# Masked aggregation of thirteen tiles instead of seven, in float32r

## The chip, the cores and the metric

The kernel runs on one core of one Trainium2 chip. The metric is the device time of one launch in microseconds. Before the change it is 1266.72 us, the median of three runs (1264.11 to 1269.66).

## The reference

A graph has 4096 nodes with 512 features each, and an integer adjacency matrix of 4096 x 4096 that has some 2 ones in a thousand and a full diagonal. Two layers are computed, each on the normalised input:

```python
h = jnp.maximum(_layernorm(x, axis=-1), 0.0)
x = x + _L0_gnn_ref(h, adj, WQ, WK, WV, we, be)
h = jnp.maximum(_layernorm(x, axis=-1), 0.0)
x = x + _L1_gnn_ref(h, adj, W_self, b_self, W_nb, b_nb, W_comb, b_comb)

# layer 0: 8 heads; attn = Q K^T / 8 + energy, masked by adj, softmax
hard = (attn == jnp.max(attn, axis=-1, keepdims=True)).astype(jnp.float32) / HEADS
out = jnp.einsum('hqk,hkd->hqd', hard, V)

# layer 1
mask = (adj > 0).astype(x.dtype)
deg = jnp.sum(mask, axis=1, keepdims=True)
agg = mask @ x / jnp.maximum(deg, 1.0)
self_f = x @ W_self + b_self
nb_f = agg @ W_nb + b_nb
out = relu(jnp.concatenate([self_f, nb_f], axis=-1) @ W_comb + b_comb)
```

The change touches only the product `mask @ x` of layer 1.

## The kernel before

The kernel works on 32 tiles of 128 nodes and keeps a second, general path for graphs that are too dense; it isn't taken here. The path that runs has three stages.

**First stage.** The adjacency matrix is read. For each node, the 4096 bits of its row are packed by matmuls into 256 words of 16 bits; word j holds the bits of the nodes j, 256 + j, 512 + j and so on. The words go to DRAM (`W_d`), and from them a list of each node's neighbours is decoded. Keys and values of layer 0 go to DRAM (`K_d`). Nodes are then ranked by their number of neighbours, and `perm` gives the new order: tile 0 holds the nodes with the longest lists. `CAPS` has the longest list of each of the 32 tiles, self included: 24, 15, 14, 13, 12, 12, 12, 11, 11, 11, 10, 10, 10, 10, 9, 9, and so on down to 5.

**Second stage.** For each tile in the new order GpSimd gathers the keys of the neighbours with indirect DMAs, VectorE scores them, and the winners' values are gathered. Layer 1's weights are folded, so that what has to be summed over neighbours is one vector of 512 per node (`gs`), which is scattered by `perm` to DRAM (`G_d`). The node's own part and its new x go to `X1_d`. Near the end of the stage the words of the first tiles are gathered (`dense_words`), turned by TensorE and copied back as integers by VectorE (`dense_turn`).

**Third stage.** The neighbours' vectors are summed, in two ways.

The first seven tiles (`DENSE = 7`) are summed by TensorE, as a product of masks and keys. There are 16 steps (`NPL`), one for each bit of the words. In step s, `dense_mask` (L1656, VectorE) shifts and masks the words of all seven tiles so that a set bit becomes the fp32 number 2.0, `dense_keys` (L1665, ScalarE's queue) loads the 256 vectors of `G_d` that belong to that bit, and `dense_sum` (L1675, TensorE) adds seven tiles x two halves of fp32 matmuls, 128x128 by 128x512, into seven PSUM banks `da0` to `da6`. Masks and keys have three buffers each.

The tiles 7 to 31 are summed from gathers: GpSimd gathers one vector per neighbour slot and node (L1110, `room<-G_d,sidx`), into a ring of three tiles' room, and VectorE sums them with one reduction (`total`, L1697; for the last tile by halves, L1706). In `finish` (L1687, L1688, VectorE) a sum is scaled by the degree and added to the node's own part, and `put` scatters the finished rows to the output (L1126, GpSimd).

The order of all this is written out by hand; each engine executes its instructions in the order of the code. A loop goes over the tiles from 7 to 31. It counts GpSimd's calls and puts the next step's mask and matmuls into the order whenever the count has passed 13 more. The first three steps stand ahead of the loop. The seven TensorE tiles are finished in iterations 27 to 29. `load_x1` (L1682, SyncE's queue) brings each tile's own part, some tiles ahead.

Of the kernel before, what the change touches and what calls it, by code (L numbers as in the profile page):

```python
# [9 lines left out]
F32 = mybir.dt.float32  # L10
BF16 = mybir.dt.bfloat16
I32 = mybir.dt.int32
AF = mybir.ActivationFunctionType
ALU = mybir.AluOpType
AX = mybir.AxisListType
# [3 lines left out]
P = 128  # L19
# [493 lines left out]
LISTV = CAPS[VTILE]  # L513
FIRST = 4
GMAX = 10
DENSE = 7
MAGIC = 0x5F3759DF


# [18 lines left out]
def sparse_path(  # L538
# [560 lines left out]
    with ExitStack() as pb:  # L1099
# [321 lines left out]
            3: [(1, NC), (0, NC)],  # L1421
        }

        def dense_words():

            wg = gp.tile([P, DENSE, SEG], F32, tag="kg", name="wg")
            for r in range(DENSE):
                gather(wg[:, r, :], W_d[:, :], perm[:, r : r + 1])
            return wg

        def dense_turn(wg):

            wT = wp.tile([P, 2, DENSE, P], I32, tag="w_a", name="wT")
            for a in range(0, DENSE, 2):
                pt = pst.tile([P, NC, P], F32, tag="tr", name="tr")
                m = min(2, DENSE - a)
                for h in range(2):
                    for b in range(m):
                        nc.tensor.transpose(pt[:, 2 * h + b, :], wg[:, a + b, ts(h, P)], ident)
                nc.vector.tensor_copy(  # L1440
                    wT[:, :, a : a + m, :],
                    pt.rearrange("p (h b) q -> p h b q", h=2)[:, :, 0:m, :],
                )
            return wT
# [87 lines left out]
        for i in range(-5, KT):  # L1532


            if i == -3:
                load_fold(0)
            if i == 0:
                load_bias()
            if i == 1:
                wS = wp.tile([P, NC, D], F32, tag="w_b", name="swS")  # L1540
                wN = bp.tile([P, NC, D], F32, tag="swN", name="swN", bufs=1)
            a, b = on(key_gathers, i), late(value_gathers, "value", i)
            while a or b:
                for q, n in ((a, max(1, round(len(a) / max(1, len(b))))), (b, 1)):
                    for g in q[:n]:
                        gather(*g)
                    del q[:n]
            on(rows, i + 5)
            late(layer1_move, "move", i)
            on(query_copy, i + 2)  # L1550
            late(layer1_copy, "layer1", i)
            early = [r for r in tail if plan["turn"][r] == i - 1]
            for r in early:
                tail_turn(r)
            if i >= 0 and turns[i] in fused:
                own_values(turns[i])
            late(layer1_stats, "stats", i)
            on(query_norm, i + 4)
            on(query, i + 1)
            for part in between.get(i, ()):  # L1560
                fold(*part)
            late(layer1, "layer1", i)
            for r in early[: -1 if i == KT - 1 else None]:
                tail_product(r)
            if i in (-2, -1, 0):
                n = 2
                for t in late_v[:n]:
# [12 lines left out]
            if i >= 0:  # L1580
                scores(turns[i], within)
            if i == KT - 2:
                wg = dense_words()
            late(scatter, "move", i)
            if i == KT - 2:
                gsl = [gp.tile([P, GRP, D], F32, tag="kg", name="gs") for _ in range(2)]
            on(winners, i)
            late(layer1_norm, "stats", i)
            on(query_turn, i + 3)
            if i < KT - 1:  # L1590
                late(layer1_turn, "turn", i)
                for r in early:
                    tail_move(r)
# [11 lines left out]
        late(layer1_norm, "stats", KT)  # L1605
        for r in early[-1:]:
            tail_move(r)
        for r in at_end:
            layer1_turn(r)
            tail_turn(r)  # L1610
# [23 lines left out]
        nc.tensor.matmul(fps, fm, ones[:, 0:1], start=True, stop=True)  # L1634
        fi = cp.tile([1, 1], I32, tag="fi", name="fi")
        nc.vector.tensor_copy(fi, fps)
        wT = dense_turn(wg)
        for r in tail:
            s = st[r]
            s["pr"] = own_product(s)  # L1640
            layer1_out(r)


    with ExitStack() as pd:
        dp = pd.enter_context(tc.tile_pool(name="sd", bufs=4))
        gp = pd.enter_context(tc.tile_pool(name="sdg", bufs=3))
        psd = pd.enter_context(tc.tile_pool(name="spsd", bufs=1, space=PSUM))
        order = pd.enter_context(ExitStack())
        order.enter_context(tc.manual_schedule())
        dacc = [psd.tile([P, D], F32, tag=f"da{r}", name="da") for r in range(DENSE)]  # L1650
        masks, keys = {}, {}

        def dense_mask(s):

            mk = gp.tile([P, 2, DENSE, P], F32, tag="mk", name="mk")
            nc.vector.tensor_scalar(  # L1656
                mk.rearrange("p h b q -> p (h b q)").bitcast(I32),
                wT.rearrange("p h b q -> p (h b q)"), 22 - s, 0x40000000,
                ALU.logical_shift_left, ALU.bitwise_and,
            )  # L1660
            masks[s] = mk

        def dense_keys(s):
            gk = gp.tile([P, 2, D], F32, tag="gk", name="gk")
            nc.scalar.dma_start(  # L1665
                gk, G_d[ds(s * SEG, SEG), :].rearrange("(h p) f -> p h f", p=P)
            )
            keys[s] = gk

        def dense_sum(s):  # L1670
            todo = [(h, r) for h in range(2) for r in range(DENSE)]
            if s == NPL - 1:
                todo.sort(key=lambda hr: hr[1])
            for h, r in todo:
                nc.tensor.matmul(  # L1675
                    dacc[r], masks[s][:, h, r, :], keys[s][:, h, :],
                    start=(s == 0 and h == 0), stop=(s == NPL - 1 and h == 1),
                )

        def load_x1(r):  # L1680
            x1 = dp.tile([P, 2, D], F32, tag="x1", name="x1", bufs=DENSE + 5)
            nc.sync.dma_start(x1, X1_d[ts(r, P), :, :])  # L1682
            return x1

        def finish(r, acc, by, x1):
            x1, y = x1[:, 0, :], x1[:, 1, :]
            nc.vector.scalar_tensor_tensor(y, acc, by, y, ALU.mult, ALU.add)  # L1687
            nc.vector.scalar_tensor_tensor(y, y, 0.0, x1, ALU.max, ALU.add)  # L1688
            done.append((r, y))

        def put():
            put_rows(out[:, :], *done.pop(0))
# [17 lines left out]
            return g[:, 0, :]  # L1710


        half = cp.tile([P, DENSE], F32, tag="half", name="half")
        nc.vector.tensor_scalar(half, smeta[:, 0:DENSE, M_RD - M_DEG], 0.5, None, ALU.mult)
        done = []
        puts.clear()
        for s in range(NPL):
            dense_keys(s)
        ahead = 3
        for s in range(ahead):  # L1720
            dense_mask(s)
            dense_sum(s)
        s = ahead
        calls = 0

        pace = 13
        x1s = {}
        for r in range(DENSE, KT):
            n = CAPS[r] - 1
            for q in [*range(r, min(r + 4, KT)), *(range(DENSE) if r == KT - 6 else ())]:  # L1730
                if q not in x1s:
                    x1s[q] = load_x1(q)
            gg = room[:, ds(r % 3 * GMAX * D, GMAX * D)].rearrange("p (n f) -> p n f", f=D)
            for i in range(n):
                gather(gg[:, i, :], G_d[:, :], sidx[:, r, i + 1 : i + 2])

            for k in range(len(done) if r == KT - 1 else 2 if r in (KT - 3, KT - 2) else 1):
                if len(done) > (r < KT - 1):
                    put()
            acc = (total if r < KT - 1 else halved)(gg, n)  # L1740
            finish(r, acc, smeta[:, r, M_RD - M_DEG : M_RD + 1 - M_DEG], x1s.pop(r))

            for k in {KT - 5: (0, 1), KT - 4: (2, 3), KT - 3: range(4, DENSE)}.get(r, ()):
                finish(k, dacc[k], half[:, k : k + 1], x1s.pop(k))
            calls += n + 1
            while s < NPL and calls >= pace * (s - 2):
                dense_mask(s)
                dense_sum(s)
                s += 1
        assert s == NPL  # L1750
        while done:
            put()
        order.close()
# [47 lines left out]
```

## Time and profile before

| what | value |
|---|---|
| median of the runs (lowest, highest) | 1266.72 us (1264.11, 1269.66) |
| span of the profiled execution | 1448.9 us |
| the profiled execution's own time | the page gives its span only |
| mean granted TensorE clock in it | 0.841 |
| busy: PE, VectorE (DVE), ScalarE (ACT), GpSimd (POOL) | 72%, 68%, 29%, 53% of the span |
| DMA | 352.57 MB, mean 243 GB/s |
| third stage | from 1128.0 us (first mask) to 1448.9 us |
| ScalarE in the third stage | no busy time |

A line of a group reads: line of the code, engine, operation, output<-inputs, shapes, count | busy us, mean ns of one | idle time of the engine just before these, and what ended most of it. PE is TensorE's matmuls and PEld its weight loads; an fp32 matmul shows as two records of each. "Remote" and "issue" are waits that the profile can't put down to an instruction. SP is SyncE. "Clock" is the share of full speed that TensorE was granted.

### The profile page before, as it was taken

The page shows a single profiled execution, that of the slowest core. Times are in us where ns is not written, and L with a number is a line of the kernel's source. Part 1 is how long each engine was busy: PE and PEld are TensorE (multiplying, and loading weights), DVE is VectorE, ACT ScalarE, POOL GpSimd, SP SyncE. Part 2 cuts the span into 40 slices and gives each one's busy share as a digit, 9 for nine tenths or more (in the row PEclk, how much of TensorE's full clock was granted, in tenths as well). Part 3 has the DMA queues.
Part 4 walks back from the last instruction along what each step waited for, and adds up shares of the span by engine and source line. Part 5 has one row for each costly group of instructions (what it writes and reads, how often), then busy time and mean ns, then how long its engine had stood idle before and what let it go on. Part 6 is the DMA issues. An engine that isn't in the chain of part 4 may idle for free.

```text
span 1448.9 us, 10626 instructions
## 1 busy us (share of the span) xinstructions
PE 1041.9 (72%) x2852; PEld 478.2 (33%) x2852; DVE 991.3 (68%) x1622; ACT 426.9 (29%) x880; POOL 772.9 (53%) x913
## 2 busy tenths in 40 slices
PE   5998989877553662754877778777895779596590
PEld 3554545433221221321332323233341334142240
DVE  5568687970990884865976878677760839487476
ACT  5787667512100420332332333333430000000000
POOL 2322322426675666544666766666527375747473
PEclk9999999989785876876978879798998789687595
DMA  9999998397754577556677777766737886757572
GB/s 365 420 419 420 419 346 301 128 365 240 210 147 120 166 222 237 177 184 188 212 221 239 243 229 225 217 211 199 263 111 237 338 263 207 246 194 257 199 246 104
DMA packets 109974, 352.57 MB, mean 243 GB/s; under 512 B 18192, under 2 KB 18192, under 8 KB 101712
## 3 DMA queue, kind: packets, MB, share of 16 engines
q0 software_dynamic: 64128, 210.72, 46.0%
q1 hardware_dynamic: 39552, 129.78, 23.2%
q10 hardware_dynamic: 6224, 11.31, 2.3%
q8 instruction: 24, 0.39, 0.1%
q14 instruction: 46, 0.38, 0.1%
HBM read 287.74 MB, written 68.19 MB: 246 GB/s over the span
## 4 chain that ended last, share of the span: by engine, by line
PE 46%; issue 19%; DVE 12%; POOL 7%; another core or an unknown queue 6%; DMA 6%; ACT 2%; SPq 0%; POOLq 0%; DVEq 0%; ACTq 0%
PE da L1675 15%; PE pg L628 7%; PE pr L1367 6%; PE q L628 5%; POOL kg L1110 4%; PE pk L628 4%; PE pv L628 3%; DVE pr L1231 3%; PE pw L768 2%; PE pr L1365 2%; POOL o L1110 2%; DMA room<-adj_dram 2%; DVE sc L1234 1%; DMA K_d<-x_dram 1%
## 5 line engine op out<-in xcount | busy, mean ns | idle before, releaser
L1675 PE MATMUL da<-gk,mk 128*128 128x512 f32 x448 | 221.7, 645 | 83.6 <-issue 56.1
L628 PE MATMUL pg<-swN,hT 128*128 128x512 f32 x216 | 133.3, 774 | 124.7 <-issue 63.7
L1110 POOL DMA_INDIRECT room<-G_d,sidx x184 | 181.1, 984 | 57.8 <-issue 54.5
L1110 POOL DMA_INDIRECT kg<-K_d,sidx x177 | 167.5, 946 | 77.9 <-issue 56.3
L628 PE MATMUL q<-wq,hqT 128*128 128x512 f32 x256 | 137.9, 670 | 70.7 <-issue 67.0
L1234 DVE TENSOR_REDUCE sc<-pr 128x32 f32<-128x2048 f32 (+3 forms) x114 | 183.3, 1608 | 5.7 <-remote 1.8
L1697 DVE TENSOR_REDUCE acc<-room 128x512 f32<-128x4096 f32 (+5 forms) x24 | 161.1, 6711 | 2.0 <-DMA room<-G_d,sidx 2.0
L1675 PEld LDWEIGHTS da<-gk,mk 128*128 128x128 f32 x448 | 91.5, 205 | 213.9 <-issue 213.9
L1110 POOL DMA_INDIRECT o<-K_d,vi x128 | 122.5, 957 | 39.3 <-issue 38.1
L628 PE MATMUL pk<-wk,room 128*128 128x512 f32 x256 | 121.7, 620 | 3.9 <-ACT room L810 3.9
L628 PEld LDWEIGHTS pg<-swN,hT 128*128 128x128 f32 x216 | 53.5, 256 | 205.1 <-issue 136.9
L628 PE MATMUL pv<-wv,room 128*128 128x512 f32 x256 | 115.7, 603 | 0.1
L1110 POOL DMA_INDIRECT room<-K_d,sidx x102 | 97.1, 952 | 32.5 <-issue 28.6
L1231 DVE TENSOR_TENSOR pr<-q,kg 128x2048 f32<-128x2048 f32 (+3 forms) x51 | 102.4, 2007 | 2.0 <-DVE sc L1234 0.7
L1367 PE MATMUL pr<-swS,hT 128*128 128x512 f32 x216 | 99.9, 605 | 0.0
L1231 DVE TENSOR_TENSOR pr<-q,room 128x2048 f32<-128x2048 f32 (+3 forms) x42 | 66.7, 1589 | 45.7 <-remote 42.7
L1126 POOL DMA_INDIRECT G_d<-gs,perm x32 | 32.5, 1017 | 122.5 <-ACT gs L1373 91.9
L628 PEld LDWEIGHTS q<-wq,hqT 128*128 128x128 f32 x256 | 51.1, 210 | 130.2 <-issue 126.9
L749 ACT ACTIVATE mkt<-adjt,sgb 128x2048 bf16<-128x2048 int32 x37 | 74.3, 2008 | 11.8 <-POOL adjt L670 11.6
L1126 POOL DMA_INDIRECT out_dram<-x,perm x32 | 33.6, 1050 | 82.5 <-DVE x L1688 51.4
L1267 DVE COPY_PREDICATED o<-best,room 128x512 f32<-128x512 int32 x102 | 74.7, 732 | 3.5
L824 POOL DMA_DIRECT2D K_d<-ks x32 | 18.8, 588 | 96.1 <-DVE ks L819 92.5
(222 smaller groups left out, 1503.4 us busy)
## 6 DMA issues: line engine op xcount, KB each, us to landing
adjt<-adj_dram SPq DMA_DIRECT2D x37, 1024.0 KB
room<-adj_dram SPq DMA_DIRECT2D x27, 1024.0 KB
x<-X_d SPq DMA_DIRECT2D x32, 512.0 KB
xt<-x_dram SPq DMA_DIRECT2D x32, 256.0 KB
K_d<-ks POOLq DMA_DIRECT2D x32, 256.0 KB
X_d<-xo SPq DMA_DIRECT2D x32, 256.0 KB
X_d<-own SPq DMA_DIRECT2D x32, 256.0 KB
gk<-G_d ACTq DMA_DIRECT2D x16, 512.0 KB
```

The costliest lines, as they stand in the source:

```text
L628: nc.tensor.matmul(dst, h[:, c, :], w[:, c, :], start=(c == 0), stop=(c == NC - 1))
L749: nc.scalar.activation(mk, st[t]["adj"][j], AF.Sigmoid, bias=sgb, scale=400.0, accum_out=degs[:, t, j : j + 1],)
L768: nc.tensor.matmul(pw, planes[:, s, :], st[t]["mk"][j][:, ts(i, SEG)], start=False, stop=(s == NPL - 1),)
L1110: last[0] = nc.gpsimd.indirect_dma_start(out=dst, out_offset=None, in_=src, in_offset=bass.IndirectOffsetOnAxis(ap=idx, axis=0), element_o ...
L1126: new = nc.gpsimd.indirect_dma_start(out=dst, out_offset=bass.IndirectOffsetOnAxis(ap=perm[:, r : r + 1], axis=0), in_=src, in_offset=None,)
L1231: nc.vector.tensor_tensor(pr[:, :g, :], s["q"].unsqueeze(1).to_broadcast([P, g, D]), kk, ALU.mult)
L1234: nc.vector.tensor_reduce(sc[:, g0 : g0 + g, :], pr[:, :g, :].rearrange("p g (h d) -> p g h d", h=H), AX.X, ALU.add,)
L1267: nc.vector.copy_predicated(s["o"].rearrange("p (h d) -> p h d", h=H), best[:, k, :].bitcast(I32).unsqueeze(2).to_broadcast([P, H, HD]), b ...
L1365: nc.tensor.matmul(pr, ones[0:1, :], bb[0:1, :], start=True, stop=False)
L1367: nc.tensor.matmul(pr, s["hT1"][:, c, :], wS[:, c, :], start=False, stop=(c == NC - 1))
L1675: nc.tensor.matmul(dacc[r], masks[s][:, h, r, :], keys[s][:, h, :], start=(s == 0 and h == 0), stop=(s == NPL - 1 and h == 1),)
L1697: nc.vector.tensor_reduce(acc, g[:, 0:n, :].rearrange("p n f -> p f n"), AX.X, ALU.add)
```

## The change

Thirteen tiles instead of seven are summed by TensorE, in two passes over the 16 bits: tiles 0 to 6, then 7 to 12. The loop over gathered tiles starts at 13. There are 32 steps; in each the 256 keys of a bit are loaded (so each is loaded twice in all).

The matmuls are in float32r, a rounded fp32. Keys are split in two float32r parts: `hi` is a copy by ScalarE, `lo` is keys minus `hi` by VectorE, and each fp32 matmul becomes two float32r matmuls into the same bank. The mask is made by VectorE as integers, as before, into a tile of its own (`mi`), and copied by ScalarE to float32r (`mk`).

Key loads move from ScalarE's queue to SyncE's, three steps ahead; loads of x1 have 11 buffers, not 12. The words of the second group are gathered ahead of the last scatters of the second stage and turned behind the last own products. PSUM banks are reused: the second pass's tiles have the banks 7 and 0 to 4, so that the first pass's tiles are finished in steps 16 and 17. Steps are put into the order for every 4.6 calls of GpSimd, puts counted as calls, two steps ahead of the loop.

```diff
-DENSE = 7
+DENSE = (7, 6)
+DTILES = sum(DENSE)
...
+        def dense_words(k):
+            n, at = DENSE[k], k * DENSE[0]
+            wg = gp.tile([P, n, SEG], F32, tag="kg", name="wg")
+            for r in range(n):
+                gather(wg[:, r, :], W_d[:, :], perm[:, at + r : at + r + 1])
             return wg
...
             if i == KT - 2:
-                wg = dense_words()
+                wgs = [dense_words(0)]
...
         late(layer1_norm, "stats", KT)
         for r in early[-1:]:
             tail_move(r)
+        wgs.append(dense_words(1))
...
-        wT = dense_turn(wg)
+        wTs = [dense_turn(0, wgs[0])]
         for r in tail:
             s = st[r]
             s["pr"] = own_product(s)
             layer1_out(r)
+        wTs.append(dense_turn(1, wgs[1]))
...
-        gp = pd.enter_context(tc.tile_pool(name="sdg", bufs=3))
+        gp = pd.enter_context(tc.tile_pool(name="sdg", bufs=2))
...
+        def dense_mask(u):
+            k, s = divmod(u, NPL)
+            shape = [P, 2, DENSE[k], P]
+            mi = gp.tile(shape, I32, tag="mi", name="mi")
             nc.vector.tensor_scalar(
-                mk.rearrange("p h b q -> p (h b q)").bitcast(I32),
-                wT.rearrange("p h b q -> p (h b q)"), 22 - s, 0x40000000,
+                mi.rearrange("p h b q -> p (h b q)"),
+                wTs[k].rearrange("p h b q -> p (h b q)"), 22 - s, 0x40000000,
                 ALU.logical_shift_left, ALU.bitwise_and,
             )
+            mk = gp.tile(shape, F32R, tag="mk", name="mk", bufs=3)
+            nc.scalar.copy(
+                mk.rearrange("p h b q -> p (h b q)"),
+                mi.rearrange("p h b q -> p (h b q)").bitcast(F32),
+            )
+            masks[u] = mk
+
+        def dense_keys(u):
+            s = u % NPL
+            gk = gp.tile([P, 2, D], F32, tag="gk", name="gk", bufs=3)
+            nc.sync.dma_start(
                 gk, G_d[ds(s * SEG, SEG), :].rearrange("(h p) f -> p h f", p=P)
             )
+            keys[u] = gk
+
+        def dense_split(u):
+            gk = keys.pop(u)
+            hi = gp.tile([P, 2, D], F32R, tag="hi", name="hi")
+            nc.scalar.copy(hi, gk)
+            lo = gp.tile([P, 2, D], F32R, tag="lo", name="lo")
+            nc.vector.tensor_tensor(lo, gk, hi.bitcast(F32), ALU.subtract)
+            keys[u] = (hi, lo)
+
+        def dense_sum(u):
+            k, s = divmod(u, NPL)
+            at = k * DENSE[0]
+            if s == 0:
+                for r in range(DENSE[k]):
+                    dacc[at + r] = psd.tile([P, D], F32, tag=f"da{(at + r) % 8}", name="da")
+            todo = [(h, r) for h in range(2) for r in range(DENSE[k])]
             if s == NPL - 1:
                 todo.sort(key=lambda hr: hr[1])
+            mk, parts = masks.pop(u), keys.pop(u)
             for h, r in todo:
-                nc.tensor.matmul(
-                    dacc[r], masks[s][:, h, r, :], keys[s][:, h, :],
-                    start=(s == 0 and h == 0), stop=(s == NPL - 1 and h == 1),
-                )
+                for c, part in enumerate(parts):
+                    nc.tensor.matmul(
+                        dacc[at + r], mk[:, h, r, :], part[:, h, :],
+                        start=(s == 0 and h == 0 and c == 0),
+                        stop=(s == NPL - 1 and h == 1 and c == 1),
+                    )
...
+        def step(u):
+            dense_mask(u)
+            if u + 3 < STEPS:
+                dense_keys(u + 3)
+            dense_split(u)
+            dense_sum(u)
+            if u == NPL - 1:
+                for r in range(DENSE[0]):
+                    load_x1(r)
+            if u == NPL:
+                for r in range(0, 4):
+                    finish_dense(r)
+            if u == NPL + 1:
+                for r in range(4, DENSE[0]):
+                    finish_dense(r)
+            if u == STEPS - 2:
+                for r in range(DENSE[0], DTILES):
+                    load_x1(r)
+
+        for u in range(3):
+            dense_keys(u)
+        for r in range(DTILES, DTILES + 3):
+            load_x1(r)
+        step(0)
+        step(1)
+        u = 2
         calls = 0
-        pace = 13
+        pace = 4.6
-        for r in range(DENSE, KT):
+        for r in range(DTILES, KT):
             n = CAPS[r] - 1
...
+            while len(done) > (1 if r < KT - 1 else 0):
+                put()
+                calls += 1
             acc = (total if r < KT - 1 else halved)(gg, n)
...
+            calls += n
+            while u < STEPS and calls >= pace * (u - 2):
+                step(u)
+                u += 1
+            if r == KT - 2:
+                while u < STEPS:
+                    step(u)
+                    u += 1
+                for k in range(DENSE[0], DTILES):
+                    finish_dense(k)
```

More of the change, by code (lines that the diff above doesn't have):

```diff
@@ L12 @@
 I32 = mybir.dt.int32
+F32R = mybir.dt.float32r
 AF = mybir.ActivationFunctionType
@@ L1422, in sparse_path, with dense_turn @@
         }
[L1424 to L1428, printed above, removed]
-            return wg
-        def dense_turn(wg):
-            wT = wp.tile([P, 2, DENSE, P], I32, tag="w_a", name="wT")
-            for a in range(0, DENSE, 2):
+        def dense_words(k):
[3 more added lines that the diff above has]
+                gather(wg[:, r, :], W_d[:, :], perm[:, at + r : at + r + 1])
+            return wg
+        def dense_turn(k, wg):
+            n = DENSE[k]
+            wT = wp.tile([P, 2, n, P], I32, tag=("w_a", "w_b")[k], name="wT")
+            for a in range(0, n, 2):
                 pt = pst.tile([P, NC, P], F32, tag="tr", name="tr")
-                m = min(2, DENSE - a)
+                m = min(2, n - a)
                 for h in range(2):
@@ L1649, in sparse_path @@
         order.enter_context(tc.manual_schedule())
-        dacc = [psd.tile([P, D], F32, tag=f"da{r}", name="da") for r in range(DENSE)]
+        dacc = {}
         masks, keys = {}, {}
-        def dense_mask(s):
-            mk = gp.tile([P, 2, DENSE, P], F32, tag="mk", name="mk")
+        STEPS = 2 * NPL
+        def dense_mask(u):
+            k, s = divmod(u, NPL)
+            shape = [P, 2, DENSE[k], P]
+            mi = gp.tile(shape, I32, tag="mi", name="mi")
             nc.vector.tensor_scalar(
-                mk.rearrange("p h b q -> p (h b q)").bitcast(I32),
-                wT.rearrange("p h b q -> p (h b q)"), 22 - s, 0x40000000,
+                mi.rearrange("p h b q -> p (h b q)"),
+                wTs[k].rearrange("p h b q -> p (h b q)"), 22 - s, 0x40000000,
@@ L1659, in dense_mask @@
                 ALU.logical_shift_left, ALU.bitwise_and,
             )
[L1661 to L1665, printed above, removed]
+            mk = gp.tile(shape, F32R, tag="mk", name="mk", bufs=3)
[8 more added lines that the diff above has]
+            nc.sync.dma_start(
@@ L1666, in dense_keys @@
                 gk, G_d[ds(s * SEG, SEG), :].rearrange("(h p) f -> p h f", p=P)
             )
-            keys[s] = gk
-        def dense_sum(s):
-            todo = [(h, r) for h in range(2) for r in range(DENSE)]
+            keys[u] = gk
[6 more added lines that the diff above has]
+            keys[u] = (hi, lo)
@@ L1680, in load_x1, with finish @@
         def load_x1(r):
-            x1 = dp.tile([P, 2, D], F32, tag="x1", name="x1", bufs=DENSE + 5)
+            x1 = dp.tile([P, 2, D], F32, tag="x1", name="x1", bufs=11)
             nc.sync.dma_start(x1, X1_d[ts(r, P), :, :])
-            return x1
-        def finish(r, acc, by, x1):
+            x1s[r] = x1
+        def finish(r, acc, by):
+            x1 = x1s.pop(r)
             x1, y = x1[:, 0, :], x1[:, 1, :]
@@ L1689, in finish, with finish_dense @@
             done.append((r, y))
+        def finish_dense(r):
+            finish(r, dacc[r], half[:, r : r + 1])
         def put():
@@ L1710, in halved @@
             return g[:, 0, :]
-        half = cp.tile([P, DENSE], F32, tag="half", name="half")
-        nc.vector.tensor_scalar(half, smeta[:, 0:DENSE, M_RD - M_DEG], 0.5, None, ALU.mult)
+        half = cp.tile([P, DTILES], F32, tag="half", name="half")
+        nc.vector.tensor_scalar(half, smeta[:, 0:DTILES, M_RD - M_DEG], 0.5, None, ALU.mult)
         done = []
         puts.clear()
[L1717 to L1723, printed above, removed]
+        x1s = {}
+        def step(u):
[23 more added lines that the diff above has]
+        u = 2
         calls = 0
-        pace = 13
-        x1s = {}
-        for r in range(DENSE, KT):
+        pace = 4.6
+        for r in range(DTILES, KT):
             n = CAPS[r] - 1
-            for q in [*range(r, min(r + 4, KT)), *(range(DENSE) if r == KT - 6 else ())]:
-                if q not in x1s:
-                    x1s[q] = load_x1(q)
+            if r + 3 < KT:
+                load_x1(r + 3)
             gg = room[:, ds(r % 3 * GMAX * D, GMAX * D)].rearrange("p (n f) -> p n f", f=D)
@@ L1735, in sparse_path @@
                 gather(gg[:, i, :], G_d[:, :], sidx[:, r, i + 1 : i + 2])
-            for k in range(len(done) if r == KT - 1 else 2 if r in (KT - 3, KT - 2) else 1):
-                if len(done) > (r < KT - 1):
-                    put()
+            while len(done) > (1 if r < KT - 1 else 0):
+                put()
+                calls += 1
             acc = (total if r < KT - 1 else halved)(gg, n)
[L1741 to L1750, printed above, removed]
+            finish(r, acc, smeta[:, r, M_RD - M_DEG : M_RD + 1 - M_DEG])
+            calls += n
[8 more added lines that the diff above has]
+                    finish_dense(k)
         while done:
```

## The prediction

> **What bounds the kernel now.** I read the page first, then its last stage (from 1128 us, where masks, keys and final sums run) as groups, stretches, waits and timeline. The page says that the profiled execution has a span of 1448.9 us and no other time; that is 182.2 us above the median of the runs, 1266.72. So I ask at once what in it a shorter execution cannot hold.
>
> The groups of the last stage (count | busy us, mean ns | idle before):
> ```profile
> L1675 PE MATMUL da<-gk,mk 128*128 128x512 f32 x448 | 221.7, 645 | 83.6 <-issue 56.1 <-DMA gk<-G_d 27.5
> L1697 DVE TENSOR_REDUCE acc<-room 128x512 f32<-128x4096 f32 (+5 forms) x24 | 161.1, 6711 | 2.0 <-DMA room<-G_d,sidx 2.0
> L1126 POOL DMA_INDIRECT out_dram<-x,perm x32 | 33.6, 1050 | 82.5 <-DVE x L1688 51.4 <-DMA x<-X_d 21.0 <-issue 6.4
> L1656 DVE TENSOR_SCALAR mk<-wT 128x1792 int32<-128x1792 int32 x16 | 17.3, 1095 | 75.2 <-remote 73.0 <-DMA X_d<-own 2.3
> ```
> An fp32 matmul is two records: 7 tiles x 2 halves x 16 planes x 2 = 448. VectorE waits 73.0 us at its masks, in four waits of 23.4, 25.2, 6.4 and 18.0 us: three mask buffers are all held by TensorE. The stretches say why (us, PE busy (records), PEld, DVE, ACT, POOL, granted clock, DMA share, GB/s):
> ```profile
> 1183.00:1197.00 14.00, 5.31 (x6) 1.36 (x6) 0.02 (x1) 0.00 (x0) 7.82 (x9) 0.59 0.67 217
> 1243.00:1271.00 28.00, 11.64 (x12) 3.16 (x11) 3.57 (x3) 0.00 (x0) 17.79 (x19) 0.51 0.68 224
> 1324.00:1365.00 41.00, 15.59 (x16) 4.45 (x16) 17.19 (x9) 0.00 (x0) 28.67 (x29) 0.52 0.75 259
> 1200.00:1240.00 40.00, 40.00 (x91) 17.54 (x90) 39.72 (x16) 0.00 (x0) 24.90 (x25) 0.97 0.68 225
> ```
> In the last, at a granted clock of 0.97, a record takes 40/91 = 0.44 us. In the first three, 83 us hold 34 records, some 15 us of work, at a clock of 0.51 to 0.59, so some 68 us are lost. A median 182 us below the span leaves no room for all such stretches (others of the kind lie at 414 to 461 us). I take the timed runs as free of them; the other reading is a rival below.
>
> Without them, the stage is set by GpSimd and VectorE. GpSimd issues one gather per 1.25 us and one put per 1.30 us in the timeline. From its first put at 1141.7 us, 154 gathers and 32 puts are 192.5 + 41.6 = 234 us, to 1376; the last put is followed by 11.4 us to the span's end, so 1387. VectorE's work is 161.1 (sums) + 1.9 (halving, last tile) + 17.3 (masks) + 46.2 (finishing: 32 x 0.69, 32 x 0.75) = 226.5 us, from 1128 to 1355. TensorE needs 448 x 0.43 = 193 us, from 1133 to 1326. So 1387 is my end of before in the timed runs, 62 us under the profiled span.
>
> **The change, part by part.**
>
> *Sums and gathers removed.* Tiles 7 to 12 go to TensorE: 57 of 184 gathers (57 x 1.25 = 71 us of GpSimd) and six sums, 3 x 8.90 + 3 x 8.05 = 50.9 us of VectorE. GpSimd then has 102 gathers and 32 puts after its first put: 169 us, to 1311. It no longer sets the end, so its gain stops where VectorE's work begins to count. DMA loses 57 x 0.262 = 14.9 MB and gains 8.4 MB of keys read twice: no cost at a share of 0.6 to 0.8.
>
> *VectorE added.* Sixteen more masks, of 1536 columns by the 1792-column row, 16 x 0.95 = 15.2 us. Thirty-two subtractions of 128x1024: the TENSOR_TENSOR of that shape takes 1217 ns (below), so 39.0 us. No row writes float32r; I bound one subtraction by 0.6 us (the mask's rate) and 2.4 us (twice the row) and take the row, which has the same operation and shape. The turn of the second words adds three copies of 0.69 us. Sum: 226.5 - 50.9 + 15.2 + 39.0 + 2.1 = 232 us. By work alone VectorE is 5 us worse.
>
> *ScalarE added, and with it a wait.* This is the step that I expect to decide. In each of 32 steps VectorE makes the integer mask, ScalarE copies it to float32r, then ScalarE copies the keys to `hi`, and only then can VectorE subtract `hi` from the keys. Both engines are fed in the order written: mask copy before key copy on ScalarE, subtraction straight behind the mask on VectorE. That VectorE doesn't step past a waiting instruction is in the trace: behind the mask that waited 25.2 us stood a sum whose gathers had long been issued. Rows for the copies:
> ```profile
> L749 ACT ACTIVATE mkt<-adjt,sgb 128x2048 bf16<-128x2048 int32 x37 | 74.3, 2008 | 11.8 <-POOL adjt L670 11.6 <-DMA adjt<-adj_dram 0.2
> L1080 ACT ACTIVATE r_tk<-r_ohr,pcol 128x1024 bf16<-128x1024 f32 x1 | 1.1, 1147 | 2.0 <-DMA K_d<-s 2.0
> L1231 DVE TENSOR_TENSOR pr<-q,room 128x1024 f32<-128x1024 f32 x4 | 4.9, 1217 | 0.0
> ```
> Between 1.15 us for 1024 and 2.01 for 2048 columns, 1792 take 1.79 and 1536 take 1.58 us. With 0.05 us for each of two hops between engines (as around the small ScalarE and VectorE steps at 1069 us), VectorE stands still for 1.79 + 1.15 + 0.10 = 3.04 us in a step of the first pass and 2.83 in the second: 16 x 5.87 = 94 us. Behind the waiting subtraction stand the next mask, the next sum and the finishing steps, and behind those GpSimd's puts and the free room slots. Nothing of VectorE's lies beside it. Bounds: 20% either way on the copies, 75 to 113 us.
>
> *TensorE.* 832 float32r records replace 448. The trace has no float32r; its nearest rows are bf16 128x512, two records of one line and the next line's start:
> ```profile
> 284.13 0.59 PE L1039 MATMUL r_pt<-r_oh,onesb 128*128 128x512 bf16 x2 [1.53 <-issue]
> 284.56 0.59 PE L1043 MATMUL r_pp<-r_oh,tri 128*128 128x512 bf16 x2
> ```
> That is 0.215 us a record; the upper bound is 0.43, one record of the fp32 pair. I take 0.215: an fp32 product spends 2 x 0.43 = 4 x 0.215, and a format for which the keys must be split in two parts should be nearer to the bf16 row than to half of an fp32 product. The Trainium skill ("FP8 and Floating Point Precision", TensorE Precision Notes) has true fp32 as four passes through the array, as the rows have it, and a reduced fp32 beside it without a time. Then a step is 28 x 0.215 = 6.0 us (5.2 in the second pass) against VectorE's 326/32 = 10.2, and TensorE is hidden; it decides only above 10.2/28 = 0.36 us a record.
>
> TensorE will now idle between steps, and that has a price in the trace, after 27.5 us of idling:
> ```profile
> 1133.92 0.34 PEld L1675 LDWEIGHTS da<-gk,mk 128*128 128x128 f32 x1 [0.52 <-issue]
> 1134.77 0.34 PEld L1675 LDWEIGHTS da<-gk,mk 128*128 128x128 f32 x1 [0.52 <-issue]
> ...
> 1137.95 0.19 PEld L1675 LDWEIGHTS da<-gk,mk 128*128 128x128 f32 x1 [0.29 <-issue]
> 1138.38 0.19 PEld L1675 LDWEIGHTS da<-gk,mk 128*128 128x128 f32 x1 [0.24 <-issue]
> ```
> For 5 us the records are 0.85 us apart, then 0.43: 2.5 us lost. Steps come in pairs, 12 us of TensorE per about 20; with a slow start each it is 14.5, still covered. The Trainium skill ("TensorE: Matmul & The Clock Gate", Part 1) speaks against this change: an idle window of about 3.4 us puts the array back to half clock, and a busy one of as much frees it. As an estimate from that page, each pair would lose 1.7 us where the row says 2.5; the sum is the same by both.
>
> *Queues and banks.* Key loads move from ScalarE's queue to SyncE's, between loads of x1. There, loads of x1 wait for puts today (longest 26.5 us), but 11 buffers hold the five that are live; only at step 15, with seven more, does one wait, and the keys behind it are needed three steps (30 us) later: nothing, or up to 20 us if that cover goes. The second pass reuses PSUM banks 0 to 4, so TensorE waits in step 16 for VectorE's finishing; step 18's `hi` waits for that, 0 to 10 us, taken as 0 because TensorE has 4 us to spare in a step. The second words put 6 gathers (7.5 us) ahead of the last two scatters, which go from 1077.0 and 1080.4 to 1081.2 and 1082.5 us: 2 us later, but the stage starts at 1128 with the landing of a store that five fewer gathers now delay. Between -4 and +2; I take 0.
>
> *Sum.* VectorE ends at 1128 + 232 + 94 = 1454, one put and the end follow, 1.3 + 11.4: 1467. Against 1387 that is +80 us: 1266.7 + 80 = 1347. Its own range, from the bounds of copies and subtraction (-39 and +57 at their ends; I don't expect both ends together), is 1318 to 1378.
>
> **The rivals.** *The low-clock stretches are in the timed runs too.* For it: they are in the one execution that is shown. Against it: the 182 us. Then before ends at 1449, and after, which gives TensorE 4 us of slack a step, at 1467: +18, so 1285; a part of the stretches gives values up to 1347.
>
> *A float32r record costs 0.43 us.* TensorE becomes the bound: 832 x 0.43 = 358 us from 1134, to 1492; finishing, halving and the last put (8 us) and the end bring 1511, +124: 1391. For it is only that no record shows the format.
>
> *The other side: ScalarE's trip doesn't reach VectorE.* If the copies ran ahead, because the order on the engines isn't the written one, VectorE has 232 us and ends at 1360 to 1368, the span at 1380: -7, so 1260. With the low-clock stretches in before alone it would be -69, 1198. It decides where VectorE's stand per step falls under about 0.4 us. Against it: in the trace both engines run in the written order throughout.
>
> **How the numbers follow.** Main case 0.61; low clock in the timed runs 0.14; dear float32r 0.08; ScalarE's trip hidden 0.13, nearly all of it faster; 0.04 for a mixture near no change. About 0.5% (6.3 us) is what a measurement of this kernel can tell from no change. Faster 0.12, same 0.05, slower 0.83. The range runs from just under the low-clock case to the dear float32r case, 1278 to 1392, and leaves out the hidden trip and the mixture (0.17).
>
> **What would show it.** Right: each subtraction on VectorE preceded by about 3 us of idle released by ScalarE's key copy, near 94 us in all; GpSimd's puts waiting for VectorE; `da` records 0.215 us apart with gaps between steps; last VectorE instruction some 326 us after the first mask. Wrong: subtractions that start at once behind their mask; `da` records 0.43 us apart without gaps; or an end set by DMA.

## The result, and the profile after

| | kernel before | changed kernel |
|---|---|---|
| median of the runs | 1267.82 us (1264.11 to 1269.66) | 1323.22 us (1322.09 to 1326.19) |
| ratio | | 1.0435, 95% interval 1.0408 to 1.0462 |
| span of the profiled execution | 1448.9 us | 1324.5 us |
| third stage, first mask to the end | 320.9 us | 327.5 us |

The change makes the kernel 55.4 us slower. The forecast was 1347 us, in a range of 1278 to 1392.

The profile of after was taken at a mean granted clock of 0.885; its span and the median agree within 2 us. That of before, at a clock of 0.841, is 181 us longer than the median. The runs of this study came from several chips. On the one of one_pass_f32r the kernel before took 1264 to 1271 us in all 7 runs, at a granted clock of 0.90. On three others none of its 34 runs was under 1400 us, the medians were 1416 to 1426 us and the clock was 0.83 to 0.85. On those three, some executions of any kernel take several per cent longer than the rest: the times and ratios below are of the others, and of the longer ones that were profiled (before_c, hi_first_b, mask_twice and both with fifteen tiles) I read the third stage alone. So below I compare times only within one chip, and else the length of the third stage.

The groups of after's third stage (count | busy us, mean ns | idle before, and what ended it):
```profile
L1705 PE MATMUL da<-hi,mk 128*128 128x512 f32 x416 | 185.5, 446 | 61.3 <-ACT hi L1688 46.1 <-DMA gk<-G_d 9.2 <-DVE x L1719 6.0
...
L1732 DVE TENSOR_REDUCE acc<-room 128x512 f32<-128x4096 f32 (+4 forms) x18 | 115.1, 6396 | 0.0
...
L1671 ACT CAST mk<-mi 128x1792 fp32r<-128x1792 f32 (+1 forms) x32 | 50.5, 1579 | 240.8 <-DVE mi L1665 178.4 <-DMA room<-G_d,sidx 31.6 <-PE da L1705 30.8
L1128 POOL DMA_INDIRECT out_dram<-x,perm x32 | 39.5, 1236 | 131.9 <-DVE x L1720 107.8 <-PE da L1705 16.2 <-DVE mi L1665 7.3
L1690 DVE TENSOR_TENSOR lo<-gk,hi 128x1024 fp32r<-128x1024 f32 x32 | 39.2, 1225 | 88.0 <-ACT hi L1688 88.0
L1688 ACT CAST hi<-gk 128x1024 fp32r<-128x1024 f32 x32 | 33.3, 1040 | 3.2 <-DMA gk<-G_d 2.3 <-PE da L1705 0.9
```
The line of L1690 (`lo`) holds the loss. VectorE stands 88.0 us ahead of its 32 subtractions, each time until ScalarE has copied the keys. In before's profile, VectorE's waits were at the masks (73.0 us); those are gone (`mi` waits for nothing but the first start). GpSimd's puts now wait 107.8 us for VectorE. VectorE never waits for a gather (0.0 at `acc`), so GpSimd's lighter work doesn't show at the end.

The whole third stage as one stretch (us, PE busy and records, PEld, DVE, ACT, POOL, granted clock, DMA share, GB/s):
```profile
997.00:1325.00 328.00, 235.17 (x832) 179.02 (x832) 230.13 (x148) 80.99 (x64) 156.65 (x155) 0.82 0.62 216
```
VectorE works 230.1 us of it; with the 88.0 us of waits that makes 318.1. ScalarE works 81.0 us, a quarter. No engine is busy for the whole stage.

One step in the timeline (start, duration, engine, operation, and in brackets the idle time ahead of it):
```profile
1038.20 1.09 DVE L1665 TENSOR_SCALAR mi<-wT 128x1792 int32<-128x1792 int32 x1
...
1039.38 1.69 ACT L1671 CAST mk<-mi 128x1792 fp32r<-128x1792 f32 x1 [11.26 <-DVE mi L1665]
...
1040.97 1.04 ACT L1688 CAST hi<-gk 128x1024 fp32r<-128x1024 f32 x1
...
1042.04 1.22 DVE L1690 TENSOR_TENSOR lo<-gk,hi 128x1024 fp32r<-128x1024 f32 x1 [2.75 <-ACT hi L1688]
```
ScalarE had stood idle for 11.26 us, and key loads held its key copies up for only 2.3 us in the whole stage (the line of L1688 above); the key copy still came last, behind the mask copy, which had to wait for VectorE's mask. So VectorE waited for a copy that waited for VectorE.

TensorE's records at the start of a pair of steps and later in it, same view:
```profile
1025.04 0.63 PE L1705 MATMUL da<-hi,mk 128*128 128x512 f32 x1
1025.47 0.63 PE L1705 MATMUL da<-lo,mk 128*128 128x512 f32 x1
...
1030.94 0.39 PE L1705 MATMUL da<-hi,mk 128*128 128x512 f32 x1
1031.17 0.40 PE L1705 MATMUL da<-lo,mk 128*128 128x512 f32 x1
1031.41 0.39 PE L1705 MATMUL da<-hi,mk 128*128 128x512 f32 x1
```
A float32r product is one record, here 0.43 us from start to start for the first 5 us after idling, 0.23 us from then on. At the other pairs the slow part is 3 to 6 us long, and at two it is absent.

### The profile page after: what moved, and what is told of

Read it like the earlier page. It is cut to its first block, busy times and chain, and to the rows that moved or that the text cites. A ratio compares the mean times of both kernels' runs of the same rounds, so it can differ in the third digit from the quotient of the medians.

```text
span 1324.5 us, 11559 instructions
## 1 busy us (share of the span) xinstructions
PE 1034.6 (78%) x3248; PEld 564.1 (43%) x3248; DVE 998.0 (75%) x1667; ACT 508.6 (38%) x944; POOL 738.4 (56%) x867
## 5 line engine op out<-in xcount | busy, mean ns | idle before, releaser
L630 PE MATMUL q<-wq,hqT 128*128 128x512 f32 x256 | 159.8, 782 | 142.1 <-DVE pr L1233 141.9
L1705 PE MATMUL da<-hi,mk 128*128 128x512 f32 x416 | 185.5, 446 | 61.3 <-ACT hi L1688 46.1
L1705 PE MATMUL da<-lo,mk 128*128 128x512 f32 x416 | 184.3, 443 | 10.6 <-DVE lo L1690 10.6
L1112 POOL DMA_INDIRECT room<-G_d,sidx x127 | 134.0, 1055 | 40.5 <-issue 35.7
L1671 ACT CAST mk<-mi 128x1792 fp32r<-128x1792 f32 (+1 forms) x32 | 50.5, 1579 | 240.8 <-DVE mi L1665 178.4
L1705 PEld LDWEIGHTS da<-hi,mk 128*128 128x128 f32 x416 | 90.9, 219 | 90.3 <-ACT hi L1688 62.3
L1732 DVE TENSOR_REDUCE acc<-room 128x512 f32<-128x4096 f32 (+4 forms) x18 | 115.1, 6396 | 0.0
L1128 POOL DMA_INDIRECT out_dram<-x,perm x32 | 39.5, 1236 | 131.9 <-DVE x L1720 107.8
L1705 PEld LDWEIGHTS da<-lo,mk 128*128 128x128 f32 x416 | 90.5, 217 | 37.5 <-DVE lo L1690 17.5
L1690 DVE TENSOR_TENSOR lo<-gk,hi 128x1024 fp32r<-128x1024 f32 x32 | 39.2, 1225 | 88.0 <-ACT hi L1688 88.0
L1233 DVE TENSOR_TENSOR pr<-q,room 128x2048 f32<-128x2048 f32 (+3 forms) x42 | 66.8, 1590 | 47.8 <-DMA room<-K_d,sidx 42.9
L630 PE MATMUL pg<-swN,hT 128*128 128x512 f32 x216 | 97.1, 592 | 0.0
```

The costliest lines, as they stand in the source:

```text
L630: nc.tensor.matmul(dst, h[:, c, :], w[:, c, :], start=(c == 0), stop=(c == NC - 1))
L1112: last[0] = nc.gpsimd.indirect_dma_start(out=dst, out_offset=None, in_=src, in_offset=bass.IndirectOffsetOnAxis(ap=idx, axis=0), element_o ...
L1128: new = nc.gpsimd.indirect_dma_start(out=dst, out_offset=bass.IndirectOffsetOnAxis(ap=perm[:, r : r + 1], axis=0), in_=src, in_offset=None,)
L1233: nc.vector.tensor_tensor(pr[:, :g, :], s["q"].unsqueeze(1).to_broadcast([P, g, D]), kk, ALU.mult)
L1671: nc.scalar.copy(mk.rearrange("p h b q -> p (h b q)"), mi.rearrange("p h b q -> p (h b q)").bitcast(F32),)
L1690: nc.vector.tensor_tensor(lo, gk, hi.bitcast(F32), ALU.subtract)
```

## The experiments

The theory is the prediction's: VectorE sets the end, and ScalarE's two copies stand in its path in each step. The rivals: TensorE sets it, GpSimd or DMA sets it, or VectorE's added work alone is the loss.

### The kernel before, profiled again: before_again, before_c

No edit.

> The kernel before, profiled once more, to see whether the low-clock stretches of its first profile (83 us for 34 records of da, mask waits of 73.0 us) belong to its usual execution. If they do not, as the prediction took it: span within 10 us of the median 1267, mask waits in the third stage under 15 us in all, third stage near 260 us from the first mask to the end, GpSimd and VectorE in turn setting the pace. If they do: the same span, but mask waits near 70 us and a third stage near 320 us.

> The kernel before, profiled on a chip where it takes 1269 us. Theory (no low-clock stretches there): mask waits under 15 us in all, third stage 255 to 270 us, GpSimd and VectorE in turn setting the pace. Otherwise: mask waits near 40 to 73 us and a third stage near 320 us, as in the two profiles so far.

Both fell on chips on which the kernel takes over 1400 us (1426.1 and 1502.2 us for these two executions), so neither shows before on a chip of 1267 us. Their third stages are 319.1 and 319.6 us, as in the first profile (320.9); the masks wait 50.8 and 50.7 us, without the first start, for 73.0 there. In before_again the profile names TensorE as what ended 11.1 us of these waits. The stretches in which TensorE's records lie 2 us apart are in all three. The second expectation's theory could not be tried.

### The key copy ahead of the mask copy: hi_first, hi_first_b, hi_first_c

```diff
-        def dense_split(u):
-            gk = keys.pop(u)
+        def dense_hi(u):
+            gk = keys[u]
             hi = gp.tile([P, 2, D], F32R, tag="hi", name="hi")
             nc.scalar.copy(hi, gk)
+            keys[u] = (gk, hi)
+
+        def dense_split(u):
+            gk, hi = keys.pop(u)
...
         def step(u):
+            dense_hi(u)
             dense_mask(u)
```

> The changed kernel with one edit: in a step ScalarE copies the keys to hi ahead of the mask copy, not behind it. Theory (VectorE waits out ScalarE's mask copy and key copy in each step): the 88.0 us of waits at lo fall to 5 to 20 us (what is left is the second step of a pair, some 0.7 us each, and the start), the time falls by 65 to 85 us, to 1238 to 1258 us. Rival 1 (TensorE sets the pace with 832 records of 0.23 us and slow starts): 1318 to 1328 us, and VectorE waits elsewhere. Rival 2 (GpSimd or DMA sets it): the same 1318 to 1328 us.

> hi_first once more, beside the changed kernel and the kernel before on one chip. Theory (ScalarE's mask copy and key copy in VectorE's path cost the changed kernel its loss): 60 to 85 us under the changed kernel in this call, and 5 to 25 us under the kernel before where that takes 1267 us. Rival (only part of the loss is the wait, the rest is more work): at or above the kernel before on a chip of 1267 us.

> hi_first, on a chip where the kernel before takes 1269 us. Theory (the wait is the whole loss): third stage 252 to 266 us, 1245 to 1262 us in all, 5 to 25 us under the kernel before. Rival (with TensorE at its clock the kernel before is GpSimd-bound and VectorE's added work cancels what GpSimd gains): within 6 us of the kernel before.

Hi_first's third stage, the subtraction's group (count | busy us, mean ns | idle before), and then the VectorE masks and subtractions of one pair of steps in its timeline:
```profile
L1694 DVE TENSOR_TENSOR lo<-gk,hi 128x1024 fp32r<-128x1024 f32 x32 | 39.1, 1221 | 22.4 <-issue 16.0 <-ACT hi L1688 6.3
```
```profile
1128.72 1.08 DVE L1665 TENSOR_SCALAR mi<-wT 128x1792 int32<-128x1792 int32 x1
1129.72 1.22 DVE L1694 TENSOR_TENSOR lo<-gk,hi 128x1024 fp32r<-128x1024 f32 x1
1130.86 1.09 DVE L1665 TENSOR_SCALAR mi<-wT 128x1792 int32<-128x1792 int32 x1
1132.51 1.23 DVE L1694 TENSOR_TENSOR lo<-gk,hi 128x1024 fp32r<-128x1024 f32 x1 [0.57 <-ACT hi L1688]
```
In this pair the first subtraction starts behind its mask at once, the second after 0.57 us. In all, VectorE waits 22.4, 26.5 and 15.1 us at the subtractions of the three profiles, where 5 to 20 had been expected; 15.0 of the 22.4 us are two waits for which the profile names nothing. The three third stages are 261.0, 264.7 and 253.6 us, 63 to 74 us under the changed kernel's 327.5 (and 324.9 in after_again). On the chip of after_again, hi_first_b takes 1366.9 us against 1430.1, 63.2 us less. The edit leaves the work of all engines and of DMA as it was (VectorE is busy for 229.1 us in hi_first, for 230.1), so none of the rivals, which go by an engine's or DMA's load, explains the fall. The order of two copies on an engine that is three quarters idle is worth more than the whole loss of 55.4 us, if it is worth as much on a chip of 1267 us; the changed kernel's third stage is much the same on both kinds. All three fell on chips where before takes over 1400 us; there the ratios to before are 0.961 (0.947 to 0.975), 0.956 (0.938 to 0.973) and 0.954 (0.942 to 0.966), all under 1, but with wide intervals, since before scatters there. That it beats before on a chip of 1267 us was not measured. From the parts one would work out 1323.2 - 63 = 1260 us, 8 us under before, little more than the 6.3 us that can be told from none.

### The mask copied twice: mask_twice

```diff
                 mi.rearrange("p h b q -> p (h b q)").bitcast(F32),
             )
+            nc.scalar.copy(
+                mk.rearrange("p h b q -> p (h b q)"),
+                mi.rearrange("p h b q -> p (h b q)").bitcast(F32),
+            )
             masks[u] = mk
```

> The changed kernel, with the mask copy on ScalarE done twice in each step, into the same tile. ScalarE is busy 81 of 328 us in the third stage, so it has the room. Theory (the copy stands in VectorE's path in full): 16 x 1.69 + 16 x 1.47 = 50.5 us more, 1366 to 1380 us, with the waits at lo near 138 us. Rivals (TensorE, GpSimd or DMA sets the pace): at most 8 us more.

The mask copy and the subtraction among the groups of mask_twice's third stage:
```profile
L1675 ACT CAST mk<-mi 128x1792 fp32r<-128x1792 f32 (+1 forms) x32 | 50.5, 1579 | 1.0
...
L1694 DVE TENSOR_TENSOR lo<-gk,hi 128x1024 fp32r<-128x1024 f32 x32 | 39.2, 1226 | 136.2 <-ACT hi L1692 114.7 <-issue 13.0 <-ACT mk L1675 8.5
```
50.5 us of copies more on ScalarE, and VectorE's wait grows from 88.0 to 136.2 us, by 48.2 (138 us had been expected). The third stage is 375.3 us, 47.8 over after's, where the rivals allowed 8. The time of the whole (1474.7 to 1556.0 us) fell on a chip of over 1400 us and says nothing of the 1366 to 1380 that I had written for the other kind.

### Without lo's matmuls: hi_only

```diff
-                for c, part in enumerate(parts):
+                for c, part in enumerate(parts[:1]):
...
-                        stop=(s == NPL - 1 and h == 1 and c == 1),
+                        stop=(s == NPL - 1 and h == 1 and c == 0),
```

> The changed kernel without the matmuls of lo (416 of the 832 float32r records are left out, so the sums keep only the hi part of the keys); lo is still computed. Theory (TensorE is hidden): within 6 us of 1323. Rival 1 (TensorE sets the pace): 416 x 0.228 = 95 us of its work go, and the time falls by 50 us or more. Rival 2 (the slow clock at the start of each pair of steps matters): a fall of 10 to 40 us.

The groups of hi_only's third stage for hi's products, the sums and the subtractions:
```profile
L1705 PE MATMUL da<-hi,mk 128*128 128x512 f32 x416 | 138.0, 499 | 153.7 <-ACT hi L1688 145.4 <-DVE x L1719 8.1
L1732 DVE TENSOR_REDUCE acc<-room 128x512 f32<-128x4096 f32 (+4 forms) x18 | 111.0, 6168 | 0.0
...
L1690 DVE TENSOR_TENSOR lo<-gk,hi 128x1024 fp32r<-128x1024 f32 x32 | 39.2, 1226 | 83.0 <-ACT hi L1688 83.0
```
Half of TensorE's records are gone and the third stage is 318.3 us, 9 us under after's; the theory allowed 6. Of the 9, 5 are at the subtractions (83.0 for 88.0) and 4 at the sums (111.0 for 115.1). Against after_again, which ran on hi_only's kind of chip, it is 6.6 us. The time of the whole, 1416.3 us, is level with before's on that chip and can't be held against 1323. TensorE does not set the end (that allowed 50 us or more); it costs VectorE a little by the way.

### The changed kernel again: after_again

> The changed kernel once more, beside the next three, since the chip of the runs before this granted TensorE a lower clock (the kernel before took 1424 us there, not 1267). Theory (low-clock stretches cost the kernel before far more than the changed one, whose TensorE has slack in the third stage): third stage from the first mask to the end 318 to 335 us whatever the chip. On a chip where the kernel before takes 1267 us: 1318 to 1328 us. On one where it takes 1424: within 30 us of it. Rival (the change's loss of 4.35% is a fixed ratio): 1.035 to 1.055 of the kernel before on any chip.

On a chip where before takes 1426.4 us, it takes 1430.1: no difference that can be told (ratio 1.0005, 0.9965 to 1.0046). Its third stage is 324.9 us, close to the 327.5 of the first chip, while before's is 319 to 321 on such chips. So the rival with a fixed ratio falls: the loss depends on the chip. The changed kernel's third stage doesn't. That before's does is worked out and not seen: after's stages ahead of the third are 1105.8 us long here for 997.0, 109 us more, and before's whole time is 159 us longer on this chip. If its earlier stages grow alike, 50 us are left for its third.

### Two passes in fp32: two_pass_fp32

```diff
-            mi = gp.tile(shape, I32, tag="mi", name="mi")
+            mk = gp.tile(shape, F32, tag="mk", name="mk", bufs=3)
...
-            )
-            mk = gp.tile(shape, F32R, tag="mk", name="mk", bufs=3)
-            nc.scalar.copy(
...
-            nc.scalar.copy(hi, gk)
-            lo = gp.tile([P, 2, D], F32R, tag="lo", name="lo")
-            nc.vector.tensor_tensor(lo, gk, hi.bitcast(F32), ALU.subtract)
-            keys[u] = (hi, lo)
+            keys[u] = (keys.pop(u),)
```

> Thirteen tiles in two passes as in the changed kernel, but in fp32: keys are not split, the mask goes straight from VectorE to TensorE, 832 records of 0.43 us. Theory (float32r is what makes room on TensorE for the second pass; without it TensorE sets the end): 358 us of matmuls, a third stage of 375 to 400 us, 50 to 75 us over the changed kernel at full clock and more where the clock is low, with VectorE waiting for mask buffers. Rival (the loss is all from the split, two passes are harmless): 20 us or more under the changed kernel.

VectorE writes the mask straight into `mk`, in fp32.

The products and the masks among the groups of its third stage:
```profile
L1695 PE MATMUL da<-gk,mk 128*128 128x512 f32 x832 | 362.3, 598 | 7.9 <-DVE x L1709 5.9 <-DMA gk<-G_d 2.0
...
L1665 DVE TENSOR_SCALAR mk<-wT 128x1792 int32<-128x1792 int32 (+1 forms) x32 | 33.2, 1042 | 143.7 <-PE da L1695 122.8 <-remote 17.3 <-issue 3.7
```
The third stage is 381.8 us with TensorE busy throughout, 54 to 57 us over the changed kernel's; the whole takes 1481.7 us against 1430.1 in after_again on the same chip. float32r is what makes room for a second pass. The run shows something more: on a chip of over 1400 us, 832 fp32 records ran 0.44 us apart in the third stage, with none of the stretches that before has there, at a granted clock of 0.98 (a stretch, columns as before):
```profile
1101.00:1468.00 367.00, 361.05 (x830) 159.18 (x831) 182.69 (x108) 0.00 (x0) 135.24 (x143) 0.98 0.54 181
```

### float32r alone, in one pass: one_pass_f32r

```diff
-DENSE = (7, 6)
+DENSE = (7,)
...
-        wgs.append(dense_words(1))
...
-        wTs.append(dense_turn(1, wgs[1]))
...
-        STEPS = 2 * NPL
+        STEPS = NPL
...
-        pace = 4.6
+        pace = 12
```

> One part of the change alone: float32r with the split of keys and ScalarE's copies in the changed order, but seven tiles in one pass, 16 steps, one for every 12 calls, 25 tiles by gathers. Theory (each step costs VectorE a subtraction of 1.2 us and a stand of 2.75 us): 226.5 + 16 x 1.22 + 16 x 2.75 = 290 us of VectorE, a third stage of 298 to 312 us from the first mask to the end. That is 35 to 50 us over the kernel before where that takes 1267 us, and 10 to 25 us under it where its low-clock stretches make it 1424 us. Rival (float32r by itself is a gain, since TensorE needs 96 us where it needed 193, and the second pass brings the loss): a third stage of 255 to 275 us.

This one fell on a chip where before takes 1269.1 us. It takes 1305.6 us, a ratio of 1.0303 (1.0272 to 1.0333), 36.5 us more, with a third stage of 310.0 us. Of the waits of that stage, the line of the subtraction (what waits, for what: us in all, times, longest):
```profile
DVE lo L1688 <- ACT hi L1686: 45.6, 16, 4.5
```
Sixteen steps cost 45.6 us of waits, half of the 88.0 that 32 steps cost. So the float32r step in this order loses by itself. Of the change's 55.4 us, the second pass with the gathers and sums that it saves adds 19, if the two results, measured apart, can be held side by side: before takes 1267.8 and 1269.1 us beside them.

### Fifteen tiles: hi_first_7_8, hi_first_7_8_c

Against hi_first:

```diff
-DENSE = (7, 6)
+DENSE = (7, 8)
...
-        pace = 4.6
+        pace = 4.2
```

> hi_first with fifteen tiles on TensorE, seven and eight, and a step for every 4.2 calls. VectorE loses two sums (8.4 + 7.5 us) and its masks of the second pass grow by 16 x 0.3 us: 11 us less. If VectorE still sets the pace: 5 to 14 us under hi_first_b. If TensorE does by then (960 records of 0.228 us are 219 us, with some 16 slow starts of 2.5 us 259 us): the same as hi_first_b or up to 15 us over.

> hi_first_7_8 on the same chip. If VectorE sets the pace in hi_first: 5 to 14 us under hi_first_c. If TensorE does: the same or up to 15 us over.

Beside hi_first_b it takes 1358.4 us against 1366.9; beside hi_first_c, 1352.7 against 1353.8. Third stages are 256.5 and 257.1 us against 264.7 and 253.6. The first pair lies in the range for VectorE as the bound, the second in the one for TensorE; a gain is not established.

## Why the prediction was right, point by point

**The step that decides** was named: ScalarE's two copies between VectorE's mask and its subtraction. Worked out at 94 us, it measured 88.0. The copies took 1.69, 1.47 and 1.04 us where the nearest rows had given 1.79, 1.58 and 1.15. Changing the order of the copies took most of it away, doubling one of them raised it by 48.2 of the copy's own 50.5 us: shown from both sides.

**VectorE's work** came out in the sum, in part by luck. Sums 115.1 us (110 expected), masks 33.0 (32.5), subtractions 39.2 (39.0), finishing 46.1 (46.2). With the halving's 1.9 the parts add up to 235 us, 5 more than expected, all of it at the sums. But neighbours on VectorE overlap a little in time, which the prediction's adding of durations left out: it is busy for 230.1 us of the stage. The two misses cancel. From the first mask to its last instruction VectorE took 319.9 us for 326.

**TensorE hidden**: right; 0.227 us a record for the 0.215 assumed, slow starts of 3 to 6 us for the 5 in before's rows, and hi_only shows that halving its work saves 9 us at most. The Trainium skill's 3.4 us ("TensorE: Matmul & The Clock Gate", Part 1) for the slow start lies at the low end of what after's rows show; the sum goes through by both.

**GpSimd freed without a gain**: right; its puts wait 107.8 us for VectorE.

**The low-clock stretches absent from the timed runs**: right for the runs of 1267 us, as far as other kernels' profiles tell; before itself was not profiled on such a chip. In after, the 32 records of a group of folded weights at 406.6 to 420.5 us run without a gap, 0.43 us each; in after_again the same group is stretched over 421 to 475 us, with single records 2.1 to 2.8 us apart. First after, then after_again (columns as above):
```profile
406.60:420.50 13.90, 13.90 (x35) 6.20 (x34) 13.66 (x8) 1.75 (x3) 10.52 (x12) 1.00 0.55 153
```
```profile
421.00:475.00 54.00, 24.79 (x37) 9.28 (x38) 16.91 (x19) 4.75 (x10) 31.26 (x33) 0.61 0.43 120
```
But I had read them as a property of the execution; by the times and clocks of before's runs they go with the chip. On chips that have them the change costs nothing that can be told (ratio 1.0005), nearer to the rival's forecast of +18 us than to my +80.

**The term that was mis-sized** is the size of the loss: +80 worked out, +55.4 measured. On the side of after 11.5 us are found: a third stage of 327.5 us for 339. Of these, 6 are VectorE's, the wait above all (88.0 for 94), and 5 lie behind its last instruction. I had taken before's 11.4 us from the last put to the end for after as well, and after has 6.3. This goes with the number of tiles on TensorE: it is 11.4 to 11.7 us in the four profiles with seven, 6.3 to 6.5 in those with thirteen, 4.8 and 5.0 with fifteen; what fills it the profiles don't show. The other 13 lie on the side of before. I gave its third stage 259 us without the stretches. 310.0 - 36.5 = 273.5 us follows from one_pass_f32r, if the two kernels' earlier stages take the same there; some 270 us follow from after_again, if before's earlier stages grow from chip to chip as after's do. No profile of before on such a chip was to be had, so which of GpSimd's or VectorE's steps takes these 11 to 14 us stays open.

**The rivals**: a record of 0.43 us was not seen except at slow starts. The hidden trip is what hi_first builds; it came out at 254 to 265 us for the third stage, where the prediction's rival had it at 252 (1380 - 1128).

## What to carry to other kernels

When a chain of small steps goes from one engine to a second and back, look at the order in which the second engine gets its work: put the copy that doesn't need the first engine's last result ahead of the one that does. ScalarE, busy for a quarter of the stage, stood in VectorE's path because of the place of its copies in the order, not because it was full. Taking work from an engine pays only up to the next one's work: by the prediction's sums GpSimd's work ended at 1376 us and VectorE's at 1355, so 21 us were to be had at most. The change gave VectorE as much work back as it took from it (230.1 us busy in the third stage for 223.4), with a wait of 88.0 us on top.

## What the runs showed of the hardware

The same 18 sums on VectorE took 115.1 us in after and in after_again, 111.0 in hi_only, 110.8 in two_pass_fp32 and 110.2 by before's rows: some 4% more where TensorE streams both float32r parts. GpSimd's puts took 1.18 to 1.34 us on average in the kernels with the subtraction on VectorE (1.24 in after) and 1.05 to 1.06 in before and two_pass_fp32, which have none. In neither case was the cause separated from what else differs. Sustained fp32 work alone does not bring on the stretches with records 2 us apart: two_pass_fp32 has none in its third stage, but has them earlier in the same execution, at 424 to 451 us. What brings them on was not found.
